# Layer 0: queries of five batches by seven products, sums of x, norms and turns put elsewhere, and two changes of order

## The chip, the core and the metric

The kernel runs on one core of a Trainium2 chip. It is one program for two transformer layers; all data are float32. Its time is the device time of one execution in microseconds, and of several executions the median is told. Engines are named as in the profile: PE (TensorE, matrix products), DVE (VectorE), ACT (ScalarE), POOL (GpSimd) and SP (SyncE, which issues most DMAs). A profile is one execution of its own; all durations below come from it.

## What is computed

Input x has 8 batches of 512 tokens with 512 features. Layer 0, the part that is changed:

```python
# attention: 16 heads of 32, causal, with biases
q = (x @ WQ_w.T + WQ_b).reshape(b, s, 16, 32).transpose(0, 2, 1, 3)   # k, v alike
scores = where(causal, -inf, einsum('bhqd,bhkd->bhqk', q, k) / sqrt(32))
out = einsum('bhqk,bhkd->bhqd', softmax(scores), v)
x = layernorm(x + out.reshape(b, s, 512) @ WO_w.T + WO_b)
# experts: 8, of which each token takes the 2 likeliest, weighted
logits = x @ gate_weight.T + x @ (2 * gate_lora_B @ gate_lora_A).T
weights, selected = top_k(softmax(logits), 2); weights /= weights.sum(-1)
gup = x @ gate_up_proj[e] + 2 * (x @ A_gup[e].T) @ B_gup[e]
h = silu(gup[:, :256]) * gup[:, 256:]
x = layernorm(x + sum over e of weight_e * (h @ down[e] + 2 * lora of down))
```

Layer 1 is attention with 8 heads of 64 in 2 key groups, without a mask, on rows divided by their norm, and then a gated network of 1408 columns with integer weights.

## The kernel before

**Batches, groups, slots.** `attention0` (L1334) goes through the 8 batches; each has 4 groups of 4 heads (128 columns), and each group 3 slots, named (group, u). With keys in tiles of 128, u = 0 holds key tile 0 (512 query columns), u = 1 tiles 1 and 3 (384 and 128), u = 2 tile 2 (256). A batch is thus 12 slots, (0,0) to (3,2). In a slot these are issued in order:

1. `scores`: four heads' scores into `sc`, four PSUM banks with one buffer; the exponential on ACT (L1573); POOL's causal select (L1583). In slots u = 2 the second half of the `sc` buffer also gets a low-rank correction of an expert's weights: ACT scales it (L846, two operations), POOL adds it to the weights (L855, two of 128x512), and DMAs bring the weights in and out through SP.
2. the thunks of `todo` for this slot: projections, products, router steps, all by PE.
3. `product` of the slot before: the weighted sums `av` on PE, and on DVE the running sum of the exponentials (L1620).
4. the thunks of `late` for this slot.
5. at u = 1 only, `normalise` of the group before: `rs` on PE (the sum over keys, L1627), its inverse (L1107 and two more on ACT, L80 and L81 on DVE), and the product with `av` (L1634 on DVE). The inverse is later multiplied into a guard value on POOL (L1110), behind the select of the next slot u = 2.

`plan(b)` fills `todo` and `late` by slot. While batch b is in its attention, batch b-1 is projected by `wo` (`project`, one token tile of 128 rows each, L1495 adds it to x), normalised, transposed for the router (`blocks`: 16 transposes by blocks of 32, four DMAs out, one back) and its logits taken (`score`); batch b-2 gets its router's choice, ranks (`dispatch`) and table (`one_hot`, `enter`).

**Order.** A scheduler orders each engine's queue by priority and dependencies; `tc.issue_after(x)` keeps what is issued under it behind instruction x in its engine's queue. Each engine runs its queue in order. `in_order` fixes PE's order as it is written.

**PSUM.** `sc` takes four banks and `av` two. All else, that is queries, keys, values, projections, `rs`, ranks, logits and tables, takes turns on the two banks named `mm`. A matmul into one of them waits until the result before the last has been read.

**Projections of x.** Query and key of a group are sums over four blocks of 128 features; `matmul_by_columns` (L67) splits each into four pieces of 32 columns, side by side on PE. The trace counts 32 matmuls of 512 columns for one query and 32 of 256 columns for one of the seven products below. Values of batches 1 to 7 are made by seven products of half blocks instead of eight (Strassen's scheme in Winograd's form): `seven_of_weights` (L784) and `seven_of_rows` (L798) make the sums of weight blocks (once) and of x blocks (each batch, four subtractions at L806), `seven(b, n)` makes product n and adds it to the blocks of the result, which lie in SBUF (L1437; n = 1 is a copy on ACT, L1440). They come in the order 1, 6, 2, 5, 3, 7, 4, six of them in batch b-1 and the last in slot (0,0) of batch b. The sums of x of batch b+1 are in `late` of slots (0,2) and (1,0), two in each.

**Rooms.** The SBUF area for the eight experts' weights holds wq, wk, wv, wo, two buffers of the transposed x, the values and all sums until the experts are loaded near the end of this stage.

**Layer 1's first pieces** are a list of thunks, one after the other with other work; the list ends with key, value, query of group 0.

The lines that name the places:

```python
for slot, last_sums in (((0, 2), False), ((1, 0), True)) if b else (((2, 1), False), ((2, 2), True)):
    late[slot].append(lambda last_sums=last_sums: row_sums(b + 1)[1](last_sums))
for n, slot in zip(ORDER, ((1, 0), (2, 0), (2, 1), (2, 2), (3, 0), (3, 2)) if b else ...):
    todo[slot].append(lambda n=n: seven(b + 1, n))
```

Of the kernel before, what the change touches and what calls it, by code (L numbers as in the profile page):

```python
# [18 lines left out]
P = 128  # L19
NB = 8  # L20
# [416 lines left out]
class Router:  # L437
# [80 lines left out]
    def choose(self, b, parts, ps, columns):  # L518
# [33 lines left out]
        first_of_largest(rest, second, self.hots[:, 1, here, :])  # L552
        nc.vector.tensor_tensor(total, top, second, ALU.add)
        nc.vector.reciprocal(total, total)
        nc.vector.tensor_tensor(self.weights[:, 0, here], top, total, ALU.mult)
        nc.vector.tensor_tensor(self.weights[:, 1, here], second, total, ALU.mult)


        self.both = small.tile([P, NT, E], F32, name="both")
# [3 lines left out]
        for t in range(1, NT):  # L563
            nc.vector.tensor_tensor(self.earlier[:, t, :], self.earlier[:, t - 1, :], self.both[:, t - 1, :], ALU.add)
        nc.vector.tensor_tensor(self.carry, self.earlier[:, NT - 1, :], self.both[:, NT - 1, :], ALU.add)

    def dispatch(self, b, ps, columns):
# [766 lines left out]
def attention0(env, guard, keep, routes, experts, dram, p_mm, tiles_ctx):  # L1334
# [9 lines left out]
    with ExitStack() as phase:  # L1344
# [15 lines left out]
        sv, t_x, t_last = (quarters(at, n) for at, n in ((EXPERT, 3), (EXPERT + 1536, 3), (2 * EXPERT + ND * 512, 1)))  # L1360
        t_x = [*(t_x[:, i] for i in range(3)), t_last[:, 0]]

        def load_w(room, i, units=slice(0, ND)):
# [58 lines left out]
        def row_sums(b):  # L1422
            return seven_of_rows(nc, xts[b], t_x)

        def seven(b, n):
            x_of, _ = row_sums(b)
            room = v_rooms[b % 2]
            ps = mm([P, 2, 256], f"ps_{n}of7")
            for s in range(2):
                for k in range(2):  # L1430
                    matmul_by_columns(nc, ps[:, s, :], x_of[n][:, k, ts(s, P)], v_of[n][:, k, :], start=k == 0, stop=k == 1)

            def block(i, j):
                return room[:, 2 * j : 2 * (j + 1), 256 * i : 256 * (i + 1)]

            def add(out, a):
                nc.vector.tensor_tensor(out, ps, a, ALU.add)  # L1437

            if n == 1:
                nc.scalar.copy(block(0, 0), ps)  # L1440
            elif n == 6:
                add(block(1, 0), block(0, 0))
            elif n == 2:
                add(block(0, 0), block(0, 0))
            elif n == 5:
                add(block(1, 1), block(1, 0))
            elif n == 3:
                add(block(0, 1), block(1, 1))
            elif n == 7:
# [41 lines left out]
        def project(b, t, out_of_heads=False):  # L1491
            ps = mm([P, D], "ps_o")
            for c in range(ND):
                (wide if out_of_heads else multiply)(ps, aoTs[b][:, c, ts(t, P)], wo[:, c, :], c)
            nc.vector.tensor_tensor(xs[b][:, t, :], ps, xs[b][:, t, :], ALU.add)  # L1495
            if t == NT - 1:
                env.layernorm(b, lambda t: router.rows[router.row_at(b, t) :][:P])

# [11 lines left out]

        def blocks(b):
            room(b)
            flat = x1Ts[b].rearrange("p k s -> p (k s)")
            for t in range(NT):
                turns.blocks(flat, t, xs[b][:, t, :])
            turns.out(flat)
            returned[0] = turns.back(flat)

# [128 lines left out]
        def plan(b):  # L1647

            todo, late = ({(g, u): [] for g in range(ND) for u in range(len(UNITS))} for _ in range(2))
            if b == 0:  # L1650
# [72 lines left out]
        for b in range(NB):  # L1723
            todo, late = plan(b)
            for g in range(ND):
# [69 lines left out]
class Attention1:  # L1795
# [83 lines left out]
    def first_pieces(self):  # L1879
# [7 lines left out]
        def blocks(tiles):  # L1887
            for t in tiles:
# [562 lines left out]
```

## Time and profile before

| | before |
|---|---|
| median of 3 runs | 2086.05 us (2085.02 to 2086.63) |
| the profiled execution's own time | 2084.99 us |
| its span | 2083.3 us |
| layer 0's attention, up to the last batch's end | about 670 us |
| one steady batch (batch 4: 339.37 to 421.14) | 81.77 us |
| PE busy in each 100 us from 0: | 94.9, 99.6, 100, 100, 100, 99.0, 97.2 us |
| queries in layer 0 (`ps_q`, 1024 matmuls) | 120.1 us busy |
| one of the seven products (`ps_1of` to `ps_7of`, 224 matmuls each) | 13.4 us busy |
| granted clock of PE, share of full speed | 0.998 |

The span is the time from the first to the last instruction in the trace; the execution's own time has some 1.7 us more around it. Busy times of PE add up what each matmul took, and neighbouring matmuls overlap, so the time that a piece of work takes from the path is better read from starts in the timeline. An entry "[0.25 <-PE ps_rank L67]" behind an instruction says that its engine was idle for 0.25 us before it and that PE's work on `ps_rank` at line 67 ended the wait. DVE's batches are full too: 62 to 77 of 100 us in this stage.

### The profile page before, as it was taken

How to read it: one execution, taken by the hardware profiler on the slowest of the kernel's cores; microseconds unless marked ns; L12 is line 12 of the kernel's file. 1: busy time of each engine (PE TensorE's matmuls, PEld its weight loads, DVE VectorE, ACT ScalarE, POOL GpSimd, SP SyncE). 2: the span in 40 equal slices, each digit the busy share in tenths (PEclk: the TensorE clock that was granted, in tenths of full speed). 3: DMA queues.
4: the chain of work that ended last, by engine and by line, in shares of the span. 5: the costliest groups of instructions: out<-in, count | busy, mean ns of one | idle time of the engine just before them, and what ended most of it. 6: DMA issues, size and time to landing. Idle time of an engine off the chain costs nothing. (4 is left out here: it accounts for less than half of the span.)

```text
span 2083.3 us, 37551 instructions
## 1 busy us (share of the span) xinstructions
PE 2058.4 (99%) x15778; PEld 1069.4 (51%) x15778; DVE 1264.3 (61%) x2047; ACT 645.3 (31%) x916; POOL 510.7 (25%) x509
## 2 busy tenths in 40 slices
PE   9999999999999999999999999999999999999998
PEld 2333333333334677764433333333335888888886
DVE  3667687686777533233158889887868644455444
ACT  2444434344344111111143333333332322222222
POOL 1344444444435121221052231232101000000000
PEclk9999999999999999999999999999999999999999
DMA  6023424415334488876432332223102311111000
GB/s 208 22 83 123 143 81 145 150 63 173 107 139 177 153 222 256 245 228 187 129 102 62 112 122 71 77 96 102 41 1 71 101 41 61 61 61 61 21 21 22
DMA packets 193059, 226.10 MB, mean 109 GB/s; under 512 B 73818, under 2 KB 139610, under 8 KB 189298
## 3 DMA queue, kind: packets, MB, share of 16 engines
q1 hardware_dynamic: 180240, 185.44, 28.3%
q0 software_dynamic: 10560, 34.61, 5.7%
q10 hardware_dynamic: 2082, 3.56, 0.6%
q8 instruction: 127, 2.08, 0.4%
q14 instruction: 50, 0.41, 0.1%
HBM read 138.88 MB, written 84.69 MB: 107 GB/s over the span
## 5 line engine op out<-in xcount | busy, mean ns | idle before, releaser
L1573 ACT ACTIVATE p<-sc 128x2048 f32<-128x2048 f32 (+1 forms) x96 | 152.4, 1587 | 175.8 <-PE sc L67 175.8
L1262 DVE SCALAR_TENSOR_TENSOR hT<-ps_u,vec,sg 128x512 f32<-128x512 f32 x88 | 65.6, 745 | 189.4 <-PE ps_u L1257 189.1
L1583 POOL TENSOR_SCALAR_AFFINE_SELECT p<-p 128x512 f32<-128x512 f32 x128 | 97.2, 771 | 307.6 <-ACT p L1573 302.0
L1273 PE MATMUL ps_f<-ffn_w,h_half 128*128 128x512 f32 x664 | 167.6, 393 | 2.8 <-DVE h_half L1268 2.0
L990 PE MATMUL ps_gu<-xrT,experts 128*128 128x256 f32 x736 | 166.6, 379 | 0.0
L1110 POOL TENSOR_TENSOR g_total<-g_total,r_inv 128x512 f32<-128x512 f32 x64 | 83.7, 1308 | 316.2 <-DVE r_inv L2007 270.6
L1620 DVE TENSOR_TENSOR p<-p 128x1536 f32<-128x1536 f32 (+2 forms) x96 | 147.8, 1539 | 17.7 <-POOL x L1593 10.0
L990 PEld LDWEIGHTS ps_gu<-xrT,experts 128*128 128x128 f32 x736 | 139.3, 190 | 35.9 <-issue 19.3
L1977 ACT ACTIVATE p<-sc 128x1024 f32<-128x1024 f32 x128 | 124.2, 1022 | 100.5 <-PE sc L67 99.2
L2007 DVE RECIPROCAL r_inv<-r_inv 128x512 f32<-128x512 f32 x32 | 107.1, 3347 | 71.6 <-ACT r_inv L1107 71.6
L1273 PEld LDWEIGHTS ps_f<-ffn_w,h_half 128*128 128x128 f32 x664 | 122.9, 188 | 34.5 <-DVE h_half L1268 7.4
L1257 PE MATMUL ps_g<-x_high,ffn_w 128*128 128x512 f32 x352 | 137.2, 390 | 0.0
L1257 PE MATMUL ps_g<-x_low,ffn_w 128*128 128x512 f32 x352 | 137.0, 389 | 0.0
L1257 PE MATMUL ps_u<-x_low,ffn_w 128*128 128x512 f32 x352 | 136.9, 389 | 0.0
L1257 PE MATMUL ps_u<-x_high,ffn_w 128*128 128x512 f32 x352 | 136.9, 389 | 0.0
L67 PE MATMUL ps_q<-experts 128*32 128x512 f32 x1024 | 120.1, 603 | 6.1 <-DMA experts<-in_xT 4.3
L67 PE MATMUL sc<-qT,kT 64*64 64x512 f32 x1024 | 124.7, 602 | 1.2 <-ACT qT L1871 0.9
L1260 ACT ACTIVATE sg<-ps_g,vec 128x512 f32<-128x512 f32 x88 | 60.6, 689 | 195.6 <-PE ps_g L1257 195.6
L1996 PE MATMUL av<-p,v 128*64 128x512 f32 x512 | 120.8, 593 | 0.0
L202 POOL TENSOR_SCALAR rstd<-mv 128x4 f32<-128x4 f32 x15 | 3.9, 262 | 461.9 <-DVE mv L201 461.9
L67 PE MATMUL ps_k<-experts 128*32 128x512 f32 x1024 | 116.4, 595 | 0.0
L67 PE MATMUL ps_o<-attn_out,aoT 128*64 128x512 f32 x512 | 116.4, 598 | 0.0
(310 smaller groups left out, 3419.2 us busy)
## 6 DMA issues: line engine op xcount, KB each, us to landing
results<-y SPq DMA_DIRECT2D x68, 256.0 KB, 2.6
pair<-xrT SPq DMA_DIRECT2D x30, 512.0 KB, 3.3
xrT<-pair SPq DMA_DIRECT2D x120, 128.0 KB, 3.9
turned<-turned SPq DMA_DIRECT2D x56, 256.0 KB, 4.1
merged<-merged SPq DMA_DIRECT2D x48, 256.0 KB, 2.4
experts<-merged SPq DMA_DIRECT2D x8, 1536.0 KB, 6.6
x<-in_x SPq DMA_DIRECT2D x8, 1024.0 KB, 8.4
merged<-in_gate_up SPq DMA_DIRECT2D x32, 256.0 KB, 3.9
```

Of the source, the lines that this page charges most:

```text
L67: nc.tensor.matmul(out[m], lhsT=lhsT[:, m], rhs=rhs, start=start, stop=stop)
L990: nc.tensor.matmul(ps[:, j, :], lhsT=w, rhs=xT[:, c, :], start=c == 0, stop=c == ND - 1)
L1110: self.nc.gpsimd.tensor_tensor(self.total, self.total, r_inv, ALU.add)
L1257: nc.tensor.matmul(ps, lhsT=w[:, ts(dc, P)], rhs=x[:, dc, :], start=(dc, i) == (0, 0), stop=(dc, i) == (ND - 1, 1))
L1262: nc.vector.scalar_tensor_tensor(hT, u, vec[:, V_SU + c : V_SU + c + 1], sg, ALU.mult, ALU.mult)
L1273: self.nc.tensor.matmul(os[t], lhsT=h[:, ts(t, P)], rhs=self.weights(2 * NHID + c), start=(c, i) == (0, 0), stop=(c, i) == (NHID - 1, 1))
L1573: nc.scalar.activation(p, sc[:, :, :width], AF.Exp, scale=scale)
L1583: select = nc.gpsimd.affine_select(out=first, in_=first, pattern=[[0, 4], [1, P]], compare_op=ALU.is_ge, fill=0.0, base=0, channel_multipl ...
L1620: nc.vector.tensor_tensor(total[:, :, P * kt :], total[:, :, P * kt :], p[:, :, at : at + w], ALU.add)
L1977: nc.scalar.activation(p, sc, AF.Exp, scale=scale)
L1996: nc.tensor.matmul(st["av"][HD * j : HD * (j + 1), :], lhsT=st["v"][:, kt, HD * j : HD * (j + 1)], rhs=p[:, j, :], start=kt == 0, stop=kt ...
L2007: nc.vector.reciprocal(r_inv, r_inv)
```

## The change

Seven things are changed; the first is the largest.

1. **Queries of batches 2 to 6 by seven products** (`seven_q`). The blocks are of `wq` (two pairs of groups by halves of the inputs) and of xT; the sums of x are those that the values use already. Four sums of wq (`q_sums`) are made once, on DVE, in batch 0's `late` slots. Product 1 is copied on ACT in four quarters with the bias; 6, 2, 5 and 4 are one addition each on DVE, 7 two, and 3 two halves with the difference of two biases. The result lies in one of two rooms instead of a tile per group. Six products of batch b+1 stand in slots (0,2), (1,1), (2,1), (3,0), (3,1), (3,2) of batch b, the last in (0,0) of b+1. Queries of those batches vanish from u = 1 slots.
2. **Key of group 1** in batches 2 to 6 goes from slot (0,2) to (0,1).
3. **Sums of x** (L806) keep their `late` slots but must stand behind the last L1634.
4. **Layer norm of a tile set**: statistics are taken after each projection, the inverse deviation on POOL at the fourth, and the rows are normalised and sent out two tiles at a time in slots (2,0) and (2,1) (for batches whose turn goes through DMA), behind the last addition from PSUM.
5. **Turns** (`blocks`): tiles 0 and 1 in slot (2,1), tiles 2 and 3 with the DMAs in (2,2), behind the last addition too; before, all four in (2,1) of `todo`.
6. **Expert 0's load** goes from batch 6, group 1, to batch 7, group 0.
7. **Two changes of order**: the four router operations that make the two weights stand behind those that count (`carry`), and layer 1's first pieces end with key, query, value.

```diff
+        s_q = [quarters(at, 1)[:, 0] for at in (2048, 2560, 2 * EXPERT + 2560, 3 * EXPERT + 2048)]
+        q_rooms = [... for a in (experts.room(0, ND), own.tile([P, ND, S], F32, name="q_odd"))]
+        def sums_of_rows(b, last):
+            with tc.issue_after(normed[0].ins):
+                row_sums(b)[1](last)
...
+        q_of = {1: q_block(0, 0), 2: q_block(0, 1), 6: s_q[1], 5: s_q[0], 7: s_q[3], 3: s_q[2], 4: q_block(1, 1)}
+        def seven_q(b, n):
+            x_of, _ = row_sums(b)
+            room = q_rooms[b % 2]
+            ps = mm([P, 2, 256], f"ps_q{n}of7")
+            for pair in range(2):
+                for k in range(2):
+                    matmul_by_columns(nc, ps[:, pair, :], q_of[n][:, pair, ts(k, P)], x_of[n][:, k, :], ...)
+            def add(out, a):
+                added[0] = nc.vector.tensor_tensor(out, ps, a, ALU.add)
+            if n == 1:
+                for g in range(ND):
+                    heads[b, g] = [room[:, g // 2, g % 2, :]]
+                    nc.scalar.activation(block(g % 2, 0)[:, g // 2, :], ps[:, g // 2, :], AF.Identity, bias=...)
+            elif n == 6:
+                add(block(1, 0), block(1, 0))
...
+            elif n == 3:
+                for pair in range(2):
+                    nc.vector.scalar_tensor_tensor(block(0, 1)[:, pair, :], ps[:, pair, :], steps[:, pair : pair + 1],
+                                                   block(1, 1)[:, pair, :], ALU.add, ALU.add)
+            elif n == 7:
+                add(block(1, 1), block(1, 1))
+                add(block(1, 0), block(1, 0))
...
-            nc.vector.tensor_tensor(xs[b][:, t, :], ps, xs[b][:, t, :], ALU.add)
+            added[0] = nc.vector.tensor_tensor(xs[b][:, t, :], ps, xs[b][:, t, :], ALU.add)
...
+            nc.vector.bn_stats(out=stats[0][:, t, :], in_=xs[b][:, t, :])
+            nc.vector.bn_aggr(out=stats[1][:, t, :], in_=stats[0][:, t, :])
             if t == NT - 1:
-                env.layernorm(b, lambda t: router.rows[router.row_at(b, t) :][:P])
+                ...  # rstd on gpsimd, as layernorm made it
+        def behind_add(thunk):
+            with tc.issue_after(added[0].ins):
+                return thunk()
...
+                for slot, which in zip(((1, 2), (2, 0), (2, 0), (2, 1)), range(4)):
+                    late[slot].append(lambda which=which: q_sums(slice(which, which + 1)))
...
+            if 2 <= b < NB - 1:
+                todo[0, 0].append(lambda: seven_q(b, ORDER[-1]))
+            if 2 <= b + 1 < NB - 1:
+                for n, slot in zip(ORDER, ((0, 2), (1, 1), (2, 1), (3, 0), (3, 1), (3, 2))):
+                    todo[slot].append(lambda n=n: seven_q(b + 1, n))
...
-                    todo[g, 0 if by_dma and ng == 0 else 1].append(lambda nb=nb, ng=ng: query(nb, ng))
-                    todo[g, 1 if by_dma and ng == 0 else 2].append(lambda nb=nb, ng=ng: key(nb, ng))
+                    if not 2 <= nb < NB - 1:
+                        todo[g, 0 if by_dma and ng == 0 else 1].append(lambda nb=nb, ng=ng: query(nb, ng))
+                    todo[g, 1 if by_dma and ng == 0 or ng == 1 and 2 <= b < NB - 1 else 2].append(lambda nb=nb, ng=ng: key(nb, ng))
...
+                for tiles_of, slot in zip(((0, 1), (2, 3)), ((2, 0), (2, 1)) if by_dma else ((1, 1), (1, 1))):
+                    late[slot].append(lambda tiles_of=tiles_of: behind_add(lambda: norm_rows(pb, *tiles_of)))
                 if by_dma:
-                    todo[2, 1].append(lambda: blocks(pb))
+                    late[2, 1].append(lambda: behind_add(lambda: blocks(pb, 0, 1)))
+                    late[2, 2].append(lambda: behind_add(lambda: blocks(pb, 2, 3)))
...
-                    late[slot].append(lambda last_sums=last_sums: row_sums(b + 1)[1](last_sums))
+                    late[slot].append(lambda last_sums=last_sums: sums_of_rows(b + 1, last_sums))
...
-                if b == NB - 2 and g == 1:
+                if b == NB - 1 and g == 0:
...
-                + [do["key"], do["value"], lambda: do["query"](0)])
+                + [do["key"], lambda: do["query"](0), do["value"]])
```

More of the change, by code (lines that the diff above doesn't have):

```diff
@@ L552, in choose @@
         first_of_largest(rest, second, self.hots[:, 1, here, :])
[L553 to L556, printed above, removed]
         self.both = small.tile([P, NT, E], F32, name="both")
@@ L565, in choose @@
         nc.vector.tensor_tensor(self.carry, self.earlier[:, NT - 1, :], self.both[:, NT - 1, :], ALU.add)
+        nc.vector.tensor_tensor(total, top, second, ALU.add)
+        nc.vector.reciprocal(total, total)
+        nc.vector.tensor_tensor(self.weights[:, 0, here], top, total, ALU.mult)
+        nc.vector.tensor_tensor(self.weights[:, 1, here], second, total, ALU.mult)
     def dispatch(self, b, ps, columns):
@@ L1361, in attention0 @@
         t_x = [*(t_x[:, i] for i in range(3)), t_last[:, 0]]
+        s_q = [quarters(at, 1)[:, 0] for at in (2048, 2560, 2 * EXPERT + 2560, 3 * EXPERT + 2048)]
+        q_rooms = [a.rearrange("p (g i) f -> p g i f", i=2) for a in (experts.room(0, ND), own.tile([P, ND, S], F32, name="q_odd"))]
         def load_w(room, i, units=slice(0, ND)):
@@ L1436, in add @@
             def add(out, a):
-                nc.vector.tensor_tensor(out, ps, a, ALU.add)
+                added[0] = nc.vector.tensor_tensor(out, ps, a, ALU.add)
             if n == 1:
@@ L1448, in seven, with q_block, q_sums @@
                 add(block(0, 1), block(1, 1))
+            elif n == 7:
+                add(block(1, 1), block(1, 1))
+                add(block(1, 0), block(1, 0))
+            else:
+                add(block(1, 0), block(1, 0))
+        def q_block(i, j):
+            return wq.rearrange("p (g i) f -> p g i f", i=2)[:, :, i, 256 * j : 256 * (j + 1)]
+        q_of = {1: q_block(0, 0), 2: q_block(0, 1), 6: s_q[1], 5: s_q[0], 7: s_q[3], 3: s_q[2], 4: q_block(1, 1)}
+        def q_sums(which):
+            for out, a, b, op in ((s_q[0], q_block(1, 0), q_block(1, 1), ALU.add), (s_q[1], s_q[0], q_block(0, 0), ALU.subtract),
+                                  (s_q[2], q_block(0, 1), s_q[1], ALU.subtract),
+                                  (s_q[3], q_block(0, 0), q_block(1, 0), ALU.subtract))[which]:
+                nc.vector.tensor_tensor(out, a, b, op)
@@ new lines, in attention0, with block @@
+        steps = own.tile([P, 2], F32, name="steps")
+        both = vec[:, V_BQ : V_BQ + ND].rearrange("p (g i) -> p g i", i=2)
+        nc.vector.tensor_tensor(steps, both[:, :, 0], both[:, :, 1], ALU.subtract)
+        def seven_q(b, n):
[4 more added lines that the diff above has]
+                for k in range(2):
+                    matmul_by_columns(nc, ps[:, pair, :], q_of[n][:, pair, ts(k, P)], x_of[n][:, k, :], start=k == 0, stop=k == 1)
+            def block(i, j):
+                return room[:, :, i, 256 * j : 256 * (j + 1)]
+            def add(out, a):
+                added[0] = nc.vector.tensor_tensor(out, ps, a, ALU.add)
+            if n == 1:
+                for g in range(ND):
+                    heads[b, g] = [room[:, g // 2, g % 2, :]]
+                    nc.scalar.activation(block(g % 2, 0)[:, g // 2, :], ps[:, g // 2, :], AF.Identity,
+                                         bias=vec[:, V_BQ + g : V_BQ + g + 1])
+            elif n == 6:
+                add(block(1, 0), block(1, 0))
+            elif n == 2:
+                add(block(0, 0), block(0, 0))
+            elif n == 5:
+                add(block(1, 1), block(1, 0))
+            elif n == 3:
+                for pair in range(2):
+                    nc.vector.scalar_tensor_tensor(block(0, 1)[:, pair, :], ps[:, pair, :], steps[:, pair : pair + 1],
+                                                   block(1, 1)[:, pair, :], ALU.add, ALU.add)
@@ L1494, in project, with norm_rows @@
                 (wide if out_of_heads else multiply)(ps, aoTs[b][:, c, ts(t, P)], wo[:, c, :], c)
-            nc.vector.tensor_tensor(xs[b][:, t, :], ps, xs[b][:, t, :], ALU.add)
-            if t == NT - 1:
-                env.layernorm(b, lambda t: router.rows[router.row_at(b, t) :][:P])
+            added[0] = nc.vector.tensor_tensor(xs[b][:, t, :], ps, xs[b][:, t, :], ALU.add)
+            if out_of_heads:
+                if t == NT - 1:
+                    env.layernorm(b, lambda t: router.rows[router.row_at(b, t) :][:P])
+                return
+            if t == 0:
+                stats[:] = env.small.tile([P, NT, 6], F32, name="stats"), env.small.tile([P, NT, 2], F32, name="mv")
+            nc.vector.bn_stats(out=stats[0][:, t, :], in_=xs[b][:, t, :])
+            nc.vector.bn_aggr(out=stats[1][:, t, :], in_=stats[0][:, t, :])
+            if t == NT - 1:
+                rstd = env.small.tile([P, NT], F32, name="rstd")
+                nc.gpsimd.tensor_scalar(rstd, stats[1][:, :, 1], LN_EPS, None, ALU.add)
+                nc.gpsimd.tensor_tensor(rstd, rstd, env.neg_half, ALU.pow)
+                stats.append(rstd)
+        def norm_rows(b, *tiles):
+            for t in tiles:
+                x = xs[b][:, t, :]
+                nc.vector.tensor_scalar(x, x, stats[1][:, t, 0:1], stats[2][:, t : t + 1], ALU.subtract, ALU.mult)
+                nc.sync.dma_start(out=router.rows[router.row_at(b, t) :][:P], in_=x)
+        def behind_add(thunk):
+            with tc.issue_after(added[0].ins):
+                return thunk()
+        stats, added = [], [None]
         x1Ts, logits = {}, {}
@@ L1509, in room, with blocks @@
             x1Ts[b] = work.tile([P, ND, S], F32, tag="x1T", name="x1T")
-        def blocks(b):
-            room(b)
+        def blocks(b, *tiles):
+            if tiles[0] == 0:
+                room(b)
             flat = x1Ts[b].rearrange("p k s -> p (k s)")
-            for t in range(NT):
+            for t in tiles:
                 turns.blocks(flat, t, xs[b][:, t, :])
-            turns.out(flat)
-            returned[0] = turns.back(flat)
+            if tiles[-1] == NT - 1:
+                turns.out(flat)
+                returned[0] = turns.back(flat)
         def turn(b, c, mm=mm):
```

## The prediction

> **What bounds the kernel now.** I read the page's busy times first, then the waits of TensorE alone, then the order of time of one steady batch (batch 4, from 339.37 to 421.14 us) engine by engine.
>
> The first line is the page's, the next two are the waits of TensorE (us in total, times, longest), and the last is the view of one source line (min/median/max in ns).
>
> ```profile
> PE 2058.4 (99%) x15778; PEld 1069.4 (51%) x15778; DVE 1264.3 (61%) x2047; ACT 645.3 (31%) x916; POOL 510.7 (25%) x509
> ...
> PE ps_q L67 <- DVE experts L1437: 1.4, 2, 1.0
> ...
> PE sc L67 <- ACT qT L1871: 0.9, 1, 0.9
> ...
> L855 POOL TENSOR_TENSOR merged<-merged,scaled x48: 1265/1771/2281, 109.8 to 588.6; 128x512 f32<-128x512 f32 x48
> ```
>
> TensorE is never out of work: in layer 0 it waits for VectorE for 1.4 us in two places. So every matmul taken away counts in full, and every new wait of TensorE does too. The timeline of TensorE (start, us, line, out<-in):
>
> ```profile
> 349.38 0.69 PE L67 MATMUL sc<-lora 16*64 16x256 f32 x16
> ...
> 359.39 1.91 PE L67 MATMUL ps_1of<-experts 128*32 128x256 f32 x32
> 361.11 0.24 PE L67 MATMUL ps_rank<-both,r_before 128*32 128x32 f32 x8
> ...
> 370.58 1.04 PE L1627 MATMUL rs<-p,ones 128*32 128x512 f32 x8
> ...
> 389.17 3.64 PE L67 MATMUL ps_q<-experts 128*32 128x512 f32 x32
> 392.63 1.91 PE L67 MATMUL ps_2of<-experts 128*32 128x256 f32 x32
> ```
>
> Starts are safer than durations, as matmuls overlap: a full query takes 392.63 - 389.17 = 3.46, a product of the seven 361.11 - 359.39 = 1.72. VectorE, GpSimd and ScalarE in the same batches:
>
> ```profile
> 343.54 1.80 DVE L806 TENSOR_TENSOR experts<-experts 128x512 f32<-128x512 f32 x1
> ...
> 357.69 1.88 DVE L1620 TENSOR_TENSOR p<-p 128x1024 f32<-128x1024 f32 x1
> 359.64 0.69 DVE L1495 TENSOR_TENSOR x<-ps_o,x 128x512 f32<-128x512 f32 x1
> ...
> 361.52 0.19 DVE L579 TENSOR_TENSOR mine<-ps_rank,r_hots 128x32 f32<-128x32 f32 x1 [0.25 <-PE ps_rank L67]
> ...
> 368.80 0.74 DVE L1477 TENSOR_SCALAR q<-ps_q,vec 128x512 f32<-128x512 f32 x1
> ...
> 418.05 2.79 DVE L1620 TENSOR_TENSOR p<-p 128x1536 f32<-128x1536 f32 x2
> ```
> ```profile
> 341.30 3.49 POOL L855 TENSOR_TENSOR merged<-merged,scaled 128x512 f32<-128x512 f32 x2
> 344.74 1.09 POOL L1583 TENSOR_SCALAR_AFFINE_SELECT p<-p 128x512 f32<-128x512 f32 x1
> ...
> 357.20 1.29 POOL L1110 TENSOR_TENSOR g_total<-g_total,r_inv 128x512 f32<-128x512 f32 x1 [4.16 <-DVE r_inv L81]
> 358.44 3.51 POOL L855 TENSOR_TENSOR merged<-merged,scaled 128x512 f32<-128x512 f32 x2
> ...
> 419.51 0.78 POOL L1583 TENSOR_SCALAR_AFFINE_SELECT p<-p 128x512 f32<-128x512 f32 x1 [3.70 <-ACT p L1573]
> ```
> ```profile
> 349.57 0.60 ACT L1107 ACTIVATE r_inv<-rs 128x512 f32<-128x512 f32 x1 [0.23 <-PE rs L1627]
> ...
> 352.22 1.07 ACT L846 ACTIVATE scaled<-sc 128x512 f32<-128x512 f32 x2
> ```
>
> Here VectorE and GpSimd stand in each other's way. L806 usually takes 0.6 from start to start; at 343.54 it took 1.80 and ended 0.6 after the GpSimd additions that ended at 344.79. The L1620 addition at 357.69 ended 1.1 after L1110's end (358.49). L855 takes 1.27 alone, and its pair 3.5 where such an addition came between. At 419.51 it went the other way: GpSimd waited for the first L1620 addition, went next, and the second addition ended 0.55 after it (420.29 to 420.84). [...]
>
> **The change, part by part.**
>
> *Matmuls.* Per batch 2 to 6, four queries (4 x 3.46 = 13.84) become seven products (7 x 1.72 = 12.04): -1.8, five times, -9.0 in all. The products run one batch ahead: batch 1 gets longer, batch 6 loses three queries and keeps one product.
>
> *Evacuations.* VectorE does 7 additions of about 0.65 and two halves instead of two queries (0.75), ScalarE four quarters instead of two (0.69): some 3.5 more for VectorE per batch, which it has (65 of 82 us busy). What counts is what waits behind them: there are two PSUM buffers for all of this.
>
> *Sums of x (L806).* Before, two of four stood in VectorE's queue ahead of L1620 and waited 5 to 7 us for xT; that made the 1.4 us of L1437 waits. These go: -1.4. In the built order of the changed kernel the four stand after L1634 of slot (0,1): three, then L1620 of 1024 elements, the fourth, then the addition L1495 of the first projection. I time this from r, the end of the sums' matmul (rs) in slot (0,1) (349.38 in the rows). ScalarE's L846 ends at r + 3.91 (353.29). The slot's key (3.46) is replaced by a product (1.72), so TensorE is ready for the next scores at 0.48 + 0.57 + 1.72 + 1.00 = 3.77 and waits 0.2 for L846, whose bank it wants; then scores 1.05, projection 3.46, product 1.72: ps_rank is wanted at r + 10.2. Its buffer is the one that L1495 must empty first. VectorE starts L80 at r + 2.06 (398.24 against 396.18), then 0.72 + 0.72 + 0.61: the first sum is ready at r + 4.1, when L1110 starts. Taking turns: L1110 to 5.4, sum 0.58, L855 1.27, sum 0.58, L855 1.27, sum 0.58, select 0.64, L1620 1.1, sum 0.6: r + 12.0, and L1495 ends at 12.7. TensorE waits **2.5**. The other end: VectorE keeps its turn through the sums; then L1495 ends at 5.4 + 1.74 + 1.1 + 0.6 + 0.69 = 9.5, and the wait is 0. I take the first, for the turn at 419.51.
>
> *The product behind the one-hots.* In slot (1,1) the next rs wants the buffer of the new product 6, whose addition stands where L1477 stood, behind the router's chain: 368.80 - 361.52 = 7.28 after L579. L579 comes at 12.7 + 0.73 + 0.2 = 13.7 (rank is done before), so the addition ends at 13.7 + 7.28 + 0.62 = 21.6. TensorE goes rank 12.75, then 1.72, product 1.72, projection 3.43, av 0.86: 20.5. It waits **1.1**. Without the 2.5 above it is 0.6; if the one-hots are not held up by GpSimd (1.9 of the 7.28, from 365.03 to 367.55), 0.
>
> *Slot (3,2).* ps_7 waits for the copy of the logits, which ScalarE makes 4.4 after rs (420.90 - 416.50), while TensorE comes at 4.3; and av is split around it: 0.1 to 0.35, I take 0.25. The additions of product q7 end 0.2 before ps_4 wants their buffer.
>
> Batches 2 to 5: 0.2 + 2.5 + 1.1 + 0.25 = 4.05 each (other end 0.45 to 1.05), **16.2** together. Batch 1 has no router chain and longer slots: 0.25.
>
> *Batch 6* has neither query nor product in slots (0,2) and (1,1). Scores wait for L846 0.8; rank is wanted at r + 9.1, L1495 ends at 12.7: 3.6; the key of slot (1,2) waits for the second projection's addition, 13.7 + 7.28 + 0.69 = 21.7 against 20.8: 0.9. Sum 5.3 (other end 1.6).
>
> *Norms and turns by two tiles.* The last two transposes move behind the addition of product 5; in batch 4's clock the four DMAs out start at about 405.6 instead of 394.93, the one back 7.5 later as now (402.43), and it lands 4.8 later (3.2 to 6.1): 418. The logits are wanted at 419.3 (in batch 6 at 417.6). I take 0 for batches 1 to 5 and 0.5 for batch 6; up to 1.1 a batch if out (8.6 once, 476.78 to 485.35) and back are both at their slowest. SP's queue behind it (x, merged tiles, xT) moves by 10; xT landed 11.4 after its issue and has some 8 us of cover before its first product.
>
> *Hidden at nothing.* Four sums of wq on VectorE in batch 0 stand before the spread of the bias, which waits 3.2 for a DMA, and two idle stretches of 2.7 and 3.9 follow; without them 2.7. Expert 0's load moves to batch 7, far ahead of its first use.
>
> *Seams.* The router's four operations come out in the same place of VectorE's built queue at the tail: 0. In layer 1's start value and query change places; the scores' 0.9 wait for the copy of qT goes, and one matmul of the value stays behind the branch: -0.65 (0 to -1.0).
>
> [...]
>
> Sum: -9.0 - 1.4 - 0.65 + 16.2 + 0.25 + 5.3 + 0.5 = **+11.2**. The profiled execution took 2084.99 (span 2083.3), so 2096.2; its median of three is 1.06 higher, 2086.05. I say **2097**.
>
> **The rivals.**
> - *VectorE keeps the port (not slower).* One mechanism, at L806 in slot (0,2): from the point where L1495 ends before r + 10.2 there is no rank wait. Then 4 x 1.05 + 0.25 + 1.6 + 0.5 - 11.05 = -4.5: 2081.5; with the one-hots free as well 2079. For it: VectorE's sums are only 0.6 long. Against: 343.54 and 419.51.
> - *Half of it.* L855 comes late (its tile or `scaled`), so only L1110 and one L855 fall between: L1495 ends about 10.8, rank waits 0.6, rs 1.0: 2.05 a batch, batch 6 about 3: 8.2 + 0.25 + 3.5 - 11.05 = +0.9: 2087. Against: L855 follows L1110 at once in the rows.
> - *The turned tile is late too.* 1.1 more in five batches: 2102. Against: the margin of 1.3 at the median.
>
> **How the numbers follow.** The forecast 0.56, own range 2091 to 2101 (rank 2.5 +- 0.7, rs 1.1 +- 0.8 in four batches); VectorE keeps the port 0.26; half of it 0.12; late tile 0.06. 0.2% is 4.2 us, about what a measurement of this kernel can tell from no change: faster is below 2081.9, slower above 2090.2. Faster: most of the first rival, 0.20. Same: its rest 0.06 and most of the second, 0.15. Slower: 0.65. The range 2080 to 2101 leaves out the lower half of the first rival and the top.
>
> **What would show it.** In the profile after: seven products per batch at 1.72; waits of ps_rank for L1495 near 2.5, four times and longer in batch 6, and of rs for the product's addition near 1; L806 at 1.8 beside L855; no wait of sc for qT. If L806 shows 0.69 there and ps_rank has no wait, the first rival is right. I am wrong also if logits wait for DMA in every batch.

## The result, and the profile after

The changed kernel took 2117.22 us (median of 4 runs, 2113.1 to 2118.8) against 2085.55: ratio 1.0147, 95% interval 1.0135 to 1.0159. The profiled execution took 2117.21, its span 2115.1, so the span grew by 31.8. Line numbers below are those of the changed kernel: the sums of x are now L804 (L806 before), the projection's addition L1549 (L1495), GpSimd's addition to the weights L853 (L855), the running sums L1699 (L1620).

The page's first line and TensorE's waits (us in total, times, longest):

```profile
PE 2065.2 (98%) x16258; PEld 1086.9 (51%) x16258; DVE 1294.2 (61%) x2082; ACT 647.9 (31%) x926; POOL 498.1 (24%) x509
```
```profile
PE ps_rank L67 <- DVE x L1549: 15.7, 5, 3.7
...
PE av L1691 <- POOL p L1662: 2.7, 2, 2.1
...
PE sc L67 <- issue: 2.1, 1, 2.1
PE ps_gu L988 <- DMA xrT<-pair: 1.8, 1, 1.8
...
PE ps_logits L515 <- DMA x1T<-turned: 1.2, 1, 1.2
```

The wait that the prediction put first is there: ps_rank waits for the first projection's addition in batches 2 to 6. Beside it stand waits that were priced at nothing. From slot (0,0) to slot (0,0), batch 1 took 88.28 (80.45 before), batches 2 to 6 took 85.01, 85.01, 87.25, 85.90 and 80.78 (before, batch 4 took 81.77 and batch 6 82.85). Of the 31.8 us, 24.2 had come by the last `rs` of layer 0's attention (662.90 before, 687.14 after); 7.6 came later.

The wait itself, in batch 4, in the timelines of VectorE, GpSimd and TensorE (start, us, line, out<-in):

```profile
372.01 0.69 DVE L1713 TENSOR_TENSOR aoT<-av,r_inv 128x512 f32<-128x512 f32 x1
372.62 4.71 DVE L804 TENSOR_TENSOR experts<-experts 128x512 f32<-128x512 f32 x3
377.25 1.65 DVE L1699 TENSOR_TENSOR p<-p 128x1024 f32<-128x1024 f32 x1
378.82 0.68 DVE L804 TENSOR_TENSOR experts<-experts 128x512 f32<-128x512 f32 x1
379.42 0.68 DVE L1549 TENSOR_TENSOR x<-ps_o,x 128x512 f32<-128x512 f32 x1
```
```profile
372.12 1.28 POOL L1108 TENSOR_TENSOR g_total<-g_total,r_inv 128x512 f32<-128x512 f32 x1 [2.02 <-DVE r_inv L81]
373.37 3.41 POOL L853 TENSOR_TENSOR merged<-merged,scaled 128x512 f32<-128x512 f32 x2
```
```profile
374.83 1.91 PE L67 MATMUL ps_1of<-experts 128*32 128x256 f32 x32
380.16 0.27 PE L67 MATMUL ps_rank<-both,r_before 128*32 128x32 f32 x8 [3.42 <-DVE x L1549]
...
380.85 1.93 PE L67 MATMUL sc<-experts,k 32*64 32x384 f32 x32
382.71 2.76 PE L67 MATMUL ps_q6of<-experts 128*32 128x256 f32 x32
```

Three sums take 4.71 where two take 1.26 beside an idle GpSimd (the run with all four in (1,1), below), and L853's pair takes 3.41 where two take 2.50 with no sums beside them (the run without group 0's additions, at 270.85): here the two engines alternate, and each of the three sums ends 0.55 after an operation of GpSimd (373.96, 375.65 and 377.33, after 373.41, 375.10 and 376.78). TensorE stands for 3.42. What follows is new: the scores take 1.93 where the same ones took 1.12 in the trace of before, the product 2.76 where its like takes 1.91. The windows around it (us, TensorE busy and matmuls, granted clock, DMA share, GB/s):

```profile
376.70:380.20 3.50, 0.08 (x8) 1.00 0.53 159
380.20:381.00 0.80, 0.80 (x32) 1.00 0.41 147
381.00:384.50 3.50, 3.50 (x52) 0.51 0.14 46
384.50:388.00 3.50, 3.50 (x48) 1.00 0.00 0
```

Behind the stall TensorE is granted half its clock for some 3.4 us, so 1.7 us of work is lost once more. It happened behind three of the five ps_rank waits (3.42, 2.92 and 3.69; not behind the two of 2.83, for which see the end) and once in layer 1. In layer 0 that is 5.1 us.

### The profile page after: what moved, and what is told of

Read it like the earlier page. It is cut to its first block, busy times and chain, and to the rows that moved or that the text cites. A ratio compares the mean times of both kernels' runs of the same rounds, so it can differ in the third digit from the quotient of the medians.

```text
span 2115.1 us, 38585 instructions
## 1 busy us (share of the span) xinstructions
PE 2065.2 (98%) x16258; PEld 1086.9 (51%) x16258; DVE 1294.2 (61%) x2082; ACT 647.9 (31%) x926; POOL 498.1 (24%) x509
## 5 line engine op out<-in xcount | busy, mean ns | idle before, releaser
L1699 DVE TENSOR_TENSOR p<-p 128x1536 f32<-128x1536 f32 (+2 forms) x96 | 145.1, 1512 | 34.1 <-PE av L1691 19.2
L1108 POOL TENSOR_TENSOR g_total<-g_total,r_inv 128x512 f32<-128x512 f32 x64 | 83.5, 1305 | 302.5 <-DVE r_inv L2097 271.6
L67 PE MATMUL ps_q<-hT,attn_qkv 128*64 128x512 f32 (+1 forms) x504 | 116.2, 596 | 0.0
```

The source lines that it names most:

```text
L67: nc.tensor.matmul(out[m], lhsT=lhsT[:, m], rhs=rhs, start=start, stop=stop)
L1108: self.nc.gpsimd.tensor_tensor(self.total, self.total, r_inv, ALU.add)
L1699: nc.vector.tensor_tensor(total[:, :, P * kt :], total[:, :, P * kt :], p[:, :, at : at + w], ALU.add)
```

## The experiments

**One part undone: the sums of x where the scheduler puts them.**

```diff
-            with tc.issue_after(normed[0].ins):
-                row_sums(b)[1](last)
+            row_sums(b)[1](last)
```

> The changed kernel with one thing undone: the sums of x (L806 of before) may again stand where the scheduler puts them, not behind L1634. Theory (the sums in slot (0,2) take turns with GpSimd and hold up the first projection's addition; TensorE's long wait then costs a second time, since its granted clock is 0.5 for some 3.5 us after the three longest of these waits): the five waits of ps_rank (15.7 us) and the three stretches at half clock (5.1 us) go, the old waits for a sum (1.4 us) may come back: 2096 to 2098 us. Rival A (the wait only moves to the next use of the two PSUM banks): rs or the next key waits instead, 2108 to 2114. Rival B (the loss lies in the later turns and in SP's queue): less than 5 us gained, 2112 or more.

2109.8 (1.0121, 1.0104 to 1.0138). The ps_rank waits went, but `ps_q4of` now waited for additions, 13.7 us in five places, and four half clocks came. VectorE shows why (batch 4):

```profile
357.60 0.69 DVE L804 TENSOR_TENSOR experts<-experts 128x512 f32<-128x512 f32 x1 [3.34 <-DMA experts<-in_xT]
358.21 1.28 DVE L1440 TENSOR_TENSOR experts<-ps_7of,experts 128x512 f32<-128x512 f32 x2
```

A sum stands in the queue ahead of product 7's additions and waits for the transposed x, which lands late. Rival A was right, by another wait than the ones it named: with the turns late the old place is bad too.

**One part undone: norms and turns as before.** The layer norm goes back into `project`, and:

```diff
-                    late[slot].append(lambda tiles_of=tiles_of: behind_add(lambda: norm_rows(pb, *tiles_of)))
-                    late[2, 1].append(lambda: behind_add(lambda: blocks(pb, 0, 1)))
-                    late[2, 2].append(lambda: behind_add(lambda: blocks(pb, 2, 3)))
+                    todo[2, 1].append(lambda: blocks(pb, 0, 1, 2, 3))
```

> The changed kernel with the layer norm and the turns put back (all four tiles normalised after the fourth projection, all four transposed in slot (2,1)). Theory: only what the late turns cost comes back, that is av's wait for the late weights and select in batches 4 and 7 (2.7 us) and the logits' wait in batch 6 (1.2): about 2113. The five ps_rank waits stay. Rival B (the loss lies in the late turns): 2100 or less.

2119.2 (1.0164, 1.0147 to 1.0181): no gain (the intervals of the two kernels overlap), where four less were expected. av's waits and the logits' went, as expected, but `rs` in slot (2,1) waited for query product 2's addition behind the layer norms, 1.8 to 1.9 in four batches. So the parts hang together: the later norms are what makes room for the products' additions.

**The two changes of order and expert 0's load put back.** The diff's lines on these three are undone (`experts.load(0)` in batch 6, group 1, again). In this run expert 0's weights land in the room that still holds batch 6's queries, so what it computes is not what the kernel computes.

> The changed kernel with the two changes of order and the load of expert 0 put back. Theory C1 (the 2.1 us wait of the scores at 1087 us and the half clock behind it, 1.7 us, come from query standing before value): the scores' 0.9 us wait comes back instead: about 2114. Theory C2 (that wait is an accident of where ScalarE's instructions lie): no change of more than 1 us by the order itself, 2116 to 2118. If the load of expert 0 was the cause of the 1.8 us wait for rows at 859 us, 1.8 less.

2112.1 (1.0128, 1.0111 to 1.0144). The 2.1 us wait in layer 1 and the half clock behind it were gone and the old 0.9 was back; av's wait in batch 7 and the 1.8 us wait for rows were gone too. But all five ps_rank waits were followed by half clock here (two of the five stretches were twice as long as the others; 11.3 us lost). Both theories leave room for this; see the last run.

**Query product 7 behind the logits.**

```diff
-                for n, slot in zip(ORDER, ((0, 2), (1, 1), (2, 1), (3, 0), (3, 1), (3, 2))):
+                for n, slot in zip(ORDER, ((0, 2), (1, 1), (2, 1), (3, 0), (3, 1))):
                     todo[slot].append(lambda n=n: seven_q(b + 1, n))
...
                 todo[(3, 2) if by_dma else (2, 1)].append(lambda: score(pb))
+            if 2 <= b + 1 < NB - 1:
+                todo[3, 2].append(lambda: seven_q(b + 1, ORDER[5]))
```

> The changed kernel with one product moved: in slot (3,2) product 7 of the queries stands behind the logits, not ahead of them (batches 1 to 5). Theory (av is split there into 6 and 10 matmuls, as ps_7 would wait for the copy of the logits, and a split costs 0.9): av is whole again, 0.9 us less in five batches: 2113. Rival (the logits come 1.7 us earlier and wait for the turned tile by DMA): the wait of the logits takes up to 1.2 us a batch: 2117 to 2120.

2114.5 (1.0139, 1.0122 to 1.0156). av was whole again, but the logits waited for the turned tile in six batches, 6.0 in all. The split that this removes, in the changed kernel:

```profile
349.36 1.04 PE L515 MATMUL ps_logits<-x1T,r_wr 128*32 128x512 f32 x8
350.22 0.82 PE L1691 MATMUL av<-p,experts 128*32 128x384 f32 x6
351.11 1.93 PE L67 MATMUL ps_7of<-experts 128*32 128x256 f32 x32
352.86 1.05 PE L1691 MATMUL av<-p,experts 128*32 128x128 f32 x10
```

av takes 0.89 + 0.98 from start to start; the same sixteen in one piece take 0.98. The matmuls of four heads start within 0.02 of each other, and here a set of three took as long as a set of four: the next set starts 0.32 later (350.22 to 350.54), in the kernel before 0.33 behind a set of four (353.88 to 354.21).

**GpSimd's additions of group 0 left out.**

```diff
                     for after, thunk in experts.pair(free, i, beside, own).items():
+                        if after == 1 + i and beside % ND == 0:
+                            continue
```

> The changed kernel, leaving out GpSimd's two additions (L855 of before) of group 0 in every batch, so that these pieces of the experts' weights go without their low-rank part. Everything else is as it was, the place of the sums too. Theory (VectorE's sums of x and GpSimd's additions take turns; alone a sum takes 0.6): the three sums behind L1634 take about 2.5 us instead of 4.7, and the ps_rank waits fall from 2.8 to 3.7 us to 0.3 to 1.2; with the stretches at half clock gone: 2102 to 2106. Rival (the sums are simply too many ahead of the projection's addition; GpSimd has no part in it): ps_rank waits over 2 us stay, 2114 or more.

2098.0 (1.0065, 1.0048 to 1.0081), 19 less without twelve GpSimd additions that no matmul waits for directly, and below the range expected. Not all of it is theirs: of the waits named above, 10.8 of ps_rank and 5.1 of half clock went, but the wait and the half clock in layer 1 and the wait for rows (5.6 together) were absent here too, as in other runs that keep the additions. The sums stand where they stood:

```profile
283.69 2.98 DVE L804 TENSOR_TENSOR experts<-experts 128x512 f32<-128x512 f32 x3
286.59 1.21 DVE L1701 TENSOR_TENSOR p<-p 128x1024 f32<-128x1024 f32 x1
287.73 0.68 DVE L804 TENSOR_TENSOR experts<-experts 128x512 f32<-128x512 f32 x1
```

Three sums take 2.98 (L1108 and a select still take a turn each), the ps_rank waits fall from 15.7 to 4.9 and no stretch at half clock is left. The turns are shown.

**Only the queries by seven:** the edits of the first two experiments together, and both changes of order undone.

> Of the change only the queries by seven products, the key's move and the load of expert 0 that must follow from the shared room; sums of x, norms, turns and both changes of order as before. Theory (matmuls give 9 us; against it stand the split of av, 0.9 in six batches, and rs waiting for product 2 behind the layer norms, 1.9 in four batches, both seen in the earlier runs, and waits for the sums of about 1.4 as before): 2088 to 2094. Rival (products on two PSUM banks cannot be evacuated whatever stands beside them): 2100 or more. Rival (the products alone give their 9 us): 2077.

2116.7 (1.0150, 1.0133 to 1.0167), as slow as the whole change. The largest wait, `rs` in slot (3,1), 10.1 us in five places, was in no expectation. On VectorE:

```profile
437.58 1.42 DVE L804 TENSOR_TENSOR experts<-experts 128x512 f32<-128x512 f32 x2 [7.48 <-DMA experts<-in_xT]
438.92 0.87 DVE L1500 SCALAR_TENSOR_TENSOR q_odd<-ps_q3of,steps,q_odd 128x256 f32<-128x256 f32 x2
```

The scheduler puts sums ahead of product 3's additions, where they wait for xT. The products bring work that TensorE needs quickly into a queue where waiting work stands.

**Only the sums of x moved, in the kernel before** (the first experiment's two lines, added there).

> The kernel before with one part of the change alone: the sums of x must stand behind L1634 in slots (0,2) and (1,0), so beside GpSimd's additions. Queries as before. Theory (turns with GpSimd: the first projection's addition ends some 13 us after rs of slot (0,1) starts, while TensorE here wants its bank at 11.7, since a key of 3.46 stands where the change has a product): ps_rank waits of 1 to 1.8 us in batches 2 to 6, the old 1.4 us go, and no stretch at half clock as the waits are short: 2089 to 2093. Rival (the place of the sums hurts only because of the shorter slot): no waits of ps_rank, 2084.

2088.8 (1.0015, 1.0005 to 1.0024). ps_rank waited 0.8 in each of five batches, 4.0 in all, and nothing ran at half clock. The place of the sums costs by itself, 3 us. Most of the rest of the 15.7 comes, as an estimate from the starts of the kernel before, from the shorter slot (0,2): 1.74 in four batches, where a product stands for a key (3.46 - 1.72), and 3.46 in batch 6, 10.4 of the 11.7.

**The sums of x at four other places.** First two in (1,2) and two in (2,2); then the same with the logits behind av (`late[3, 2]`), expert 0 loaded a group later and layer 1's old order.

```diff
-                for slot, last_sums in (((0, 2), False), ((1, 0), True)) if b else ...:
+                for slot, last_sums in (((1, 2), False), ((2, 2), True)) if b else ...:
```

> The changed kernel with the sums of x moved only: two in late (1,2) and two in late (2,2), behind L1634 of their slots, and of the query products 2 ahead of 6, so that no sum is needed before slot (2,0). Theory (the cause is that the sums stand ahead of the first projection's addition and want a transposed x that lands late): the ps_rank waits and the half clock go and do not come back as waits of ps_q4: 2094 to 2099. Rival (the wait only moves on, as it did when the sums went back to their old place): 2105 or more.

> The same, and three more: logits behind av in slot (3,2), so that av is not split (0.9 in six batches), expert 0 loaded one group later with experts 1, 2 and 4 (the 2.1 us wait of av for the late weights in batch 7), and layer 1's old order of value and query (2 to 4 us). Theory: all that the runs named is gone but 0.5 a batch for rs: 2082 to 2088, near or just under the kernel before. Rival (turns that end late make the logits or xT wait instead): 2090 or more.

2122.1 (1.0174, 1.0157 to 1.0191) and 2130.6 (1.0209, 1.0192 to 1.0226), both worse. `ps_6of` waited for the sums, which now came just before it, and `ps_3of` for additions behind the second pair, 1.35 and 1.4 in each of six batches. The wait of `ps_6of` also split the scores beside it into 14 and 18 matmuls, some 0.85 more (in batch 3 1.90 instead of 1.05). The logits' wait for the turned tile reached 4.2. The moved logits waited 2.0 in each of five batches for something that the trace doesn't name, av waited 4.4 once, and five stretches at half clock came.

Then all four in (1,1), behind the second projection's addition, with query product 2 ahead of 6:

```diff
-            with tc.issue_after(normed[0].ins):
+            with tc.issue_after(added[0].ins if b > 1 else normed[0].ins):
...
-                for slot, last_sums in (((0, 2), False), ((1, 0), True)) if b else ...:
+                for slot, last_sums in (((1, 1), False), ((1, 1), True)) if b else ...:
...
-                for n, slot in zip(ORDER, ((0, 2), (1, 1), (2, 1), ...)):
+                for n, slot in zip((1, 2, 6, 5, 3, 7), ((0, 2), (1, 1), (2, 1), ...)):
```

> The changed kernel with only the sums of x moved: all four in late (1,1), behind the second projection's addition, where GpSimd is idle and VectorE has slack before the third; of the query products 2 ahead of 6. Theory: the ps_rank waits (15.7) and the half clock behind them (5.1) go and nothing takes their place: 2094 to 2099. Rival (the four sums, 2.4 us, hold up what follows, as they did in late (1,2) and (2,2)): waits of rs, the key or the table's bank of over 1 us a batch: 2102 or more.

2088.8 (1.0020, 1.0011 to 1.0030): 28 us from one move and the order of two products, more than expected, as the waits in layer 1 and for rows were absent too. The sums beside an idle GpSimd:

```profile
377.28 0.68 DVE L1549 TENSOR_TENSOR x<-ps_o,x 128x512 f32<-128x512 f32 x1
377.88 0.68 DVE L804 TENSOR_TENSOR experts<-experts 128x512 f32<-128x512 f32 x1
379.08 0.67 DVE L804 TENSOR_TENSOR experts<-experts 128x512 f32<-128x512 f32 x1
379.76 1.26 DVE L804 TENSOR_TENSOR experts<-experts 128x512 f32<-128x512 f32 x2
```

**av held together.** Here `made[0]` is the last matmul of a product; the scores of slot (0,0) are kept behind it in the same way, and layer 1's order is the old one.

```diff
-                        waiting()
+                        with tc.issue_after(made[0].ins) if (g, u) == (3, 2) and b < NB - 1 else ExitStack():
+                            waiting()
```

> The same, and av of slot (3,2) kept behind product 7 of the values, so that it isn't split (0.9 in five batches, against 0.1 to 0.4 of waiting for the logits' copy), and layer 1's old order of value and query (2 to 4 us). Theory: 2087 to 2092. Rival (the wait for the logits' copy is as long as the split): 2092 to 2095.

2090.1 (1.0022, 1.0013 to 1.0031): a time in the theory's range, but the rival's mechanism. `ps_7of` now waited 0.7 in each of five batches for the logits' copy, nearly as long as the split had cost (0.89), and layer 1's old order cost its 0.9.

**One-hots behind product 2, expert 0's load behind the last piece to be merged.**

```diff
+        def hots(b):
+            one_hot(b - 2, (0, 1))
+            with tc.issue_after(second[b + 1].ins):
+                return one_hot(b - 2, (2, 3))
...
-                    with behind_return():
+                    with tc.issue_after(experts.last_load.ins):
                         experts.load(0)
```

> The same again, and the last eight of the sixteen one-hots behind the addition of query product 2 (rs waits 0.5 to 0.8 a batch for it), and expert 0's load behind the last load of a piece to be merged (2 us of av in batch 7). Theory: 4 us less than the run before it: 2082 to 2088, about the kernel before. Rival (the second half of the one-hots then makes the second projection's addition late): the same as the run before it or slower.

2085.6 (1.0000, 0.9991 to 1.0009). `rs` no longer waited in (1,1) (from its scores to the next slot's first matmul 8.06 in batches 2 to 5, against 8.37 to 8.81 in the run before), and batch 7's wait of av was gone. That wait came from the order of the DMAs in SP's queue, as the changed kernel shows:

```profile
599.04 0.33 SPq L116 DMA_DIRECT2D x1T<-turned  x1
...
603.17 0.33 SPq L824 DMA_DIRECT2D experts<-merged  x1
608.71 1.62 SPq L851 DMA_DIRECT2D merged<-in_down  x2
```
```profile
615.07 2.51 POOL L853 TENSOR_TENSOR merged<-merged,scaled 128x512 f32<-128x512 f32 x2 [7.95 <-DMA merged<-in_down]
617.54 1.80 POOL L1662 TENSOR_SCALAR_AFFINE_SELECT p<-p 128x512 f32<-128x512 f32 x3
```

The turned tile is fetched late, the load of expert 0 goes next, the pieces to be merged after it; L853 waits for them, and three selects stand behind L853. From the issue of these pieces to L853 it takes 6.36 (608.71 to 615.07); with the load of expert 0 behind them, in this run, it takes 2.92 (586.65 to 589.57).

**Waits of graded length in the kernel before.**

```diff
+            with tc.issue_after(normed[0].ins):
+                for n in {2: (304,), 3: (404,), 4: (488,), 5: (290, 290), 6: (380, 380)}[b]:
+                    nc.vector.reciprocal(spare[:, 1, :n], spare[:, 0, :n])
```

> The kernel before with nothing of the change, but a reciprocal of its own on VectorE behind L1634 of slot (0,2) in batches 2 to 6, of growing width (304, 404, 488, 2x290, 2x380 columns; L2007 took 3.35 us for 512, so about 2.0, 2.7, 3.2, 3.8 and 5.0 us), so that the first projection's addition is late and ps_rank waits some 1.2, 1.9, 2.4, 3.0 and 4.2 us. It prices a wait of TensorE by its length, without queries by seven. Theory (a wait also drops the granted clock to 0.5 for 3.4 us when it is long): no half clock behind the first one or two, 1.7 us lost behind the last two at least; in all 12.7 + 3.4 to 6.8 + what else waits: 2101 to 2106. Rival (the half clock belongs to the changed kernel's denser work, not to waits): no half clock anywhere, 2097 to 2099.

2099.2 (1.0067, 1.0051 to 1.0083). The waits of ps_rank came out shorter than planned, 0.45, 1.69, 0.67, 2.27 and 4.06, so the time tells little; the windows of batch 6 do:

```profile
535.00:537.20 2.20, 0.00 (x0) 0.98 0.63 169
537.20:540.60 3.40, 3.39 (x60) 0.51 0.14 49
540.60:545.00 4.40, 4.40 (x44) 1.00 0.00 0
```

Half clock behind the 4.06 and behind none of the others, in a kernel without the change. The rival falls: here a wait brought it without the change.

**Product 7 of the values in slot (0,0) of the next batch,** instead of av held together; then the same with layer 1's new order.

```diff
+                for n in ORDER[-1 if b == 1 else -2:]:
+                    todo[0, 0].append(lambda n=n: seven(b, n))
...
-                for n, slot in zip(ORDER, ((1, 0), (2, 0), (2, 1), (2, 2), (3, 0), (3, 2)) if b else ...):
+                for n, slot in zip(ORDER, ((1, 0), (2, 0), (2, 1), (2, 2), (3, 0)) if b else ...):
```

> The run with the last one-hots behind query product 2, but with product 7 of the values moved from slot (3,2) to (0,0) of the next batch instead of av held whole. Theory (the 0.7 to 0.9 us a batch that remain in (3,2) are there because three results want two PSUM banks and the logits' copy is late; the matmul saving of 1.7 a batch is then left whole): 5 less than 2085.6: 2079 to 2082. Rival (slot (0,0) then has three products for two banks and waits for VectorE's additions there): 2084 to 2090.

> The same with layer 1's changed order (key, query, value). Theory C2 (the order by itself gains most of the 0.9 us wait of the scores for qT; the 2 to 4 us lost in some runs come from ScalarE's copy of the next qT starting 2 to 3 us late for a reason that no semaphore in the trace shows): 0.5 to 1 us less than the run before it, or 2 to 4 us more if the late copy shows up. Rival C1 (the order itself costs): always slower than the run before it.

2081.8 (0.9982, 0.9973 to 0.9991) and 2081.2 (0.9980, 0.9971 to 0.9989): the last is 4.2 us faster than the kernel before and 36 faster than the changed one, with the same matmuls. Two steady batches in its windows (TensorE's busy time and matmuls first, then weight loads, VectorE, ScalarE, GpSimd, clock):

```profile
181.19:261.63 80.44, 80.32 (x1276) 34.06 (x1272) 62.02 (x122) 35.30 (x47) 37.80 (x35) 1.00 0.40 122
261.63:342.06 80.43, 80.31 (x1276) 34.00 (x1272) 61.73 (x122) 35.29 (x47) 38.14 (x35) 1.00 0.38 118
```

The new order removes the scores' 0.86 wait for qT in the trace; between the two medians the gain is 0.5, within the spread of the runs. So the trace shows the gain that was predicted; the times agree with it, but don't show it by themselves.

## Why the prediction was wrong

The sign and the first mechanism were right; the sum, +11.2, was a third of what came. Term by term:

- **Matmuls, -1.8 a batch and -9.0 in all: right within 0.3 a batch.** A steady batch of the last run is 1.34 shorter than batch 4 before (80.43 against 81.77), of which it loses 0.2 to the wait for L844 in slot (0,2).
- **L1437 waits, -1.4: right,** they are gone.
- **ps_rank 2.5 four times and 3.6: right in mechanism, a little small:** 2.83, 2.83, 3.42, 2.92 and 3.69, 15.7 instead of 13.6. GpSimd's turns cause most of it, as the run without its additions shows (4.9 of the 15.7 were left). That the size is near is partly luck, as two errors nearly cancel: in batch 2 the first sum started 5.7 after r (201.23 - 195.55), not 4.1, and from there to the addition's end it took 7.5 (201.23 to 208.72), not 8.6.
- **rs 1.1 four times, and 0.9 for batch 6's key: too much,** 0.55 in batches 2 and 3 and none in 4 to 6, 1.1 instead of 5.3. In those three TensorE had just run at half clock and came later. Batch 6's scores waited 0.15 for L844, not 0.8.
- **The step that failed: a wait was priced at its own length.** The prediction says of what counts in full "every new wait of TensorE does too", and its sum adds the waits alone. The half clock behind them was no term of it: 5.1 in layer 0 and 1.7 in layer 1.
- **Slot (3,2), "I take 0.25": mis-sized,** 0.89 in five batches, 4.4 instead of 1.25. The copy's wait was priced; the split of av, seen in the built order, was not counted as lost parallel work.
- **The turned tile, 0 and 0.5: nearly right for the logits (1.2), wrong for "SP's queue behind it moves by 10" at nothing:** av waited 2.1 in batch 7 for the late pieces to be merged and 0.6 in batch 4. That chain was not followed from SP's queue to GpSimd's selects.
- **Layer 1's order, -0.65: right alone** (-0.86 in the trace), but in the changed kernel 2.1 of waiting and 1.7 of half clock came a few us later. There ScalarE's copy of the next qT began at 1086.38, after 5.36 idle, though its matmuls ended at about 1083.1; the row names no semaphore of this core's engines. It was there in three traces with the new order, absent in five others with it, and in none with the old order. Why is open.
- **What remains.** To the last `rs` of layer 0's attention the terms make -9.0 - 1.4 + 15.7 + 1.1 + 1.0 (L844, 0.2 in five batches) + 4.4 + 5.1 + 1.2 + 2.7, and 0.6 by which batch 1 began later: 21.4 of 24.2. The rest may be the 0.2 beside each wait (slot (1,0) grew by 3.05 for a wait of 2.83). Of the 7.6 behind it, 3.0 is layer 1's order (2.12 + 1.71 - 0.86) and 1.8 the wait for rows at 859 us, whose cause was not tried alone; the rest is small pieces that were not followed up.

The rival that VectorE keeps the port is dead: three sums took 4.71 beside GpSimd's operations and 2.98 without its additions. The port in its name was an assumption of the author's; what the two engines share, no trace shows. The third rival, late turned tiles, was there in small (1.2 in one batch).

## What to carry to other kernels

In these runs a wait of TensorE of 1.8 to 2.9 us was followed by half clock in 15 of 38 cases, which cost up to 1.7 us more where it lasted 3.4. So the place of a few VectorE operations decided more than the matmuls saved: 28 us against 9. Before moving work in a full queue, write down what the engine beside it does at that moment (three sums took 4.71 beside GpSimd's additions, 2.98 without them) and what is queued behind, and look for a slot in which both are idle. An edit that saves matmuls is tried with several placements before it is judged: the same products were 1.5% slower and 0.2% faster.

## What the hardware showed

Over all 17 traces, TensorE's waits of over 1 us in layer 0's attention (from 100 us on) and the granted clock behind them:

| length of the wait | waits | followed by half clock |
|---|---|---|
| 1.0 to 1.8 us | 62 | 0 |
| 1.8 to 2.9 us | 38 | 15 |
| 2.9 us and more | 14 | 14 |

Of the 29 stretches at half clock, 23 last 3.4 us and cost up to 1.7; six last 6.8 and cost 2.5 to 3.4. Each begins within about 2 us of the wait's end. Equal waits in one trace differ (2.32 four times: twice yes, twice no), and their place in time tells them apart. In the trace of the changed kernel the half clock begins at 381.02, 466.36, 551.69 and 1087.58 and lasts 3.413 each time; the starts are 85.33, 85.33 and 535.89 apart, 25, 25 and 157 times 3.413. In the six other traces with more than one stretch between 100 and 700 us, the starts lie whole multiples of 3.413 us apart too, within 0.02. The waits can so be sorted by how long TensorE was idle inside one window of this grid. Of the windows at full clock between 100 and 690 us, the next one ran at half clock in all 27 with 1.96 us idle or more, in 2 of the 14 with 1.72 to 1.86, and in none with less. The shortest wait with half clock behind it was 1.84 us (1.77 idle in its window, in the run with only the queries by seven). Two of the four waits of 2.32, by windows of the grid, in the run with norms and turns as before (us, TensorE busy and matmuls, granted clock, DMA share, GB/s):

```profile
205.51:208.93 3.42, 1.09 (x38) 1.00 0.56 159
208.93:212.34 3.41, 3.41 (x63) 0.50 0.28 74
...
290.84:294.25 3.41, 2.92 (x44) 1.00 0.41 139
294.25:297.67 3.42, 1.59 (x56) 1.00 0.55 168
297.67:301.08 3.41, 3.41 (x66) 1.00 0.02 5
```

The first wait lies in one window; the second is cut by a boundary into 0.49 and 1.83, and nothing follows. Why six stretches last a second window was not worked out.

VectorE's sums and GpSimd, both with work queued, took turns operation by operation: three sums 4.71 beside L1108 and two L853, 2.98 beside L1108 and a select. Two other pairs ran side by side: in the run without group 0's additions, L1486 took 0.69 (at 271.05) beside two L853 that took 2.50 (from 270.85), and in the kernel before L200 took 0.70 (at 360.36) while L855, begun at 360.67, took 1.28.
